# Where a block's shared chunk of edge slots stands among its parts

## The chip, the cores and the metric

The kernel runs on one core of a Trainium2 chip. The time is that of the device in microseconds (us) for one execution, the median of several runs. A profile of one execution gives the start and length of every instruction.

## The reference

Four graph layers run one after another on `x`, 16 graphs of 1024 nodes with 128 features, all with one adjacency matrix `adj` of 1024 x 1024, in which about one entry in 128 is set. Layers 0, 2 and 3 are masked attention with 8 heads of 16 features, followed by a feed-forward part; layer 1 is graph attention with one head.

```
# layers 0, 2, 3
Q, K, V = h @ Wq, h @ Wk, h @ Wv                     # 8 heads of 16
scores  = where(adj == 0, -inf, Q K^T / 4)
x = layer_norm(h + softmax(scores) V @ Wo + bo)
x = layer_norm(x + relu(x @ W1 + b1) @ W2 + b2)
# layer 1
h = x @ W
e = leaky_relu(h @ a_src [i] + h @ a_dst [j], 0.2)
y = softmax(where(adj == 0, -inf, e)) @ h + x
x = layer_norm(y)
```

## The kernel before

The kernel uses that `adj` is sparse. At the start it sorts the nodes by their number of edges and builds, for each node, the list of its neighbours. After that it never forms a 1024 x 1024 score matrix: for each node it gathers the rows of its neighbours from a table in HBM and works on these.

**Blocks.** The nodes are cut into T = 8 tiles of 128, and the 16 graphs into GR = 2 groups of 8. A block (the kernel says unit) is one layer l, one group g and one tile t; there are 4 x 2 x 8 = 64, in this order (L841). A tile has four quarters of 32 nodes. Edge slots of a quarter are gathered in chunks: one chunk covers S = 4 slots of the 32 nodes of one quarter j, so 128 rows on 128 partitions. `CAPS` (L61) holds how many slots each quarter of each tile needs. What is left over after the division by four, at most four slots in all quarters of a tile together, makes one more chunk, the shared one, called `MIX` in the code. It holds slots of two or three quarters.

**Parts.** L92 to L96 set the order in which the chunks of a tile are worked on. L94 lists the chunks (j, r) by their row r, and within a row in the order of quarters 0, 2, 1, 3; L95 makes pairs of neighbours in this list; L96 puts the shared chunk in as a part of its own, at place 3 when one counts from 0. In attention each entry of `PIECES` is a part. In layer 1 L847 packs neighbouring entries into one part as long as it has at most J = 4 chunks. Tile 0 has six entries, tiles 1 to 6 five, tile 7 four. For example, the order of tile 3 is (0,0)(2,0) | (1,0)(3,0) | (0,1)(2,1) | shared | (1,1)(3,1), and in layer 1 the first two of these go together, then the third with the shared chunk, then the last.

**The steps.** The loop at L1160 takes one part i per step and issues work for several parts, by hand (`manual_schedule`):
- L958 (`products`, VectorE): gathered keys times the queries. For ordinary parts the queries are `qr`; for the shared part they are `qx`, which L922 (`shared`) copies together from `qr` by DMA on SP's queue. There is one `qx` buffer.
- L1025 (`summed`, TensorE): part i-2's weighted values, 128 x 1024 for each chunk, are summed over slots by a matmul with a 128 x 32 matrix of marks, which writes to the 32 partitions of quarter j. L1035 to L1038 let a part wait and be summed with the next one, if both have the same row r and neither is shared.
- L981, L985 (`exponentials`, VectorE and ScalarE): scores and their exponentials. In layer 1 these are L990, L994 and L997.
- L1009 (`weighted`, VectorE): part i-1's gathered values times their weights. In attention it writes over the products, in the same buffer.
- L946 (`gathered`, GpSimd): the gathers of part i+3, one indirect DMA for each chunk, into one of four buffers `e`. The buffer is that of part i-1 and is free when L1009 of that part is done.

Product buffers `pr` are four too: L958 of a part needs the sum four parts earlier to be done. The sums of a block go to one accumulator `acc`. After the last part of a block, `divided` (L1053) sums the weights (`den`, also L1025), takes the reciprocal (L1062) and divides (L1065), which is issued in the next block's second step. Then the tails of the block (L703 for attention, L756 for layer 1: projections, layer norms, feed-forward, the table rows of the next layer) are drawn in small pieces between the steps by `others` (L1099), at an even pace. The queries of the next block (`queries`, L880) and the loads are drawn in the same way.

## Time and profile before

| what | value |
| --- | --- |
| median of 3 runs | 2261.7 us (2255.61 to 2262.03) |
| the profiled execution | 2254.23 us |
| its span, first to last instruction | 2251.9 us |
| gathers of edges, L946 | 576, mean 1483 ns on GpSimd, median 8.1 us from issue to landing |
| L958, two chunks / shared chunk | 192 of 2300 ns / 48 of 1219 ns |
| L1009, two chunks / one chunk | 256 of 2291 ns / 64 of 1217 ns |
| L981, two chunks / one chunk | 192 of 2286 ns / 48 of 1220 ns |
| L1025 into `acc` | 2624 of 608 ns, busy 519.1 us |
| DMA | 636.05 MB, mean 282 GB/s |

A row of the profile names line, engine, operation, output and inputs; a time in brackets behind a line of the timeline is the engine's idle time ahead of it, with what ended it. `PE` is TensorE, `DVE` VectorE, `ACT` ScalarE, `POOL` GpSimd and `SP` the engine that issues the other DMAs. `L1025` is busy 519.1 us though its 2624 instructions last 608 ns each, since those on different column groups run beside each other. All times in the timeline count from the start of the span.

### The profile page before, as it was taken

To read this page: it belongs to the slowest core of one execution; us is meant where nothing else is said; L and a number is where in the kernel's file an instruction comes from. 1 tells how busy PE (TensorE), PEld (TensorE's weight loads), DVE (VectorE), ACT (ScalarE), POOL (GpSimd) and SP (SyncE) were. 2 spreads that over 40 slices of the span, in tenths; PEclk is the share of its full clock that TensorE was granted. 3 is DMA by queue.
4 is the path that set the end of the run, shared out by engine and by line. 5 is a ranking of instruction groups with operands and counts; after the bars stand their busy time and mean duration, and the time that the engine had idled before them with its cause. 6 is when DMAs were issued, how large, how long until landed. Compare 5 with 4: busy or idle time off the path is not lost.

```text
span 2251.9 us, 36507 instructions
## 1 busy us (share of the span) xinstructions
PE 2043.1 (91%) x13140; PEld 1271.3 (56%) x13140; DVE 1872.9 (83%) x1472; ACT 1528.3 (68%) x5041; POOL 1016.3 (45%) x699
## 2 busy tenths in 40 slices
PE   6589999899999999998999989999999998998986
PEld 5456665555555555554556655656655555555554
DVE  7897899888887577768988889989798998888893
ACT  3346777777777655555677777777777777676765
POOL 3343445354435368884343434334444544453540
PEclk8799999999999999999999999999999998999999
DMA  7897877778788699997997978887888788687860
GB/s 254 290 323 275 298 272 279 268 263 289 284 296 272 221 341 356 360 358 291 327 329 268 318 260 302 303 313 276 284 282 305 265 286 279 225 279 271 288 227 21
DMA packets 164700, 636.05 MB, mean 282 GB/s; under 512 B 34568, under 2 KB 37384, under 8 KB 116014
## 3 DMA queue, kind: packets, MB, share of 16 engines
q0 software_dynamic: 88720, 485.08, 61.0%
q1 hardware_dynamic: 75792, 148.57, 19.1%
q8 instruction: 105, 1.72, 0.3%
q14 instruction: 83, 0.68, 0.1%
HBM read 581.08 MB, written 92.34 MB: 299 GB/s over the span
## 4 chain that ended last, share of the span: by engine, by line
PE 41%; ACT 18%; issue 16%; DVE 11%; DMA 9%; POOL 5%; POOLq 0%; DVEq 0%; ACTq 0%
PE acc L1025 9%; DMA e<-table,idx 8%; PE yps L746 5%; PE ps L576 4%; POOL e L946 4%; PE ps L646 4%; ACT qr L912 4%; PE ps L732 3%; PE ps L909 3%; DVE pr L958 3%; ACT z L624 3%; DVE sc L981 3%; DVE pr L1009 2%; PE yps L750 2%; ACT z L639 2%
## 5 line engine op out<-in xcount | busy, mean ns | idle before, releaser
L946 POOL DMA_INDIRECT e<-table,idx x576 | 854.1, 1483 | 1101.8 <-DVE pr L1009 902.1
L1009 DVE TENSOR_TENSOR pr<-e,ex 128x2048 f32<-128x2048 f32 (+1 forms) x320 | 661.6, 2076 | 46.7 <-ACT ex L985 24.9
L958 DVE TENSOR_TENSOR pr<-e,qr 128x2048 f32<-128x2048 f32 x192 | 441.6, 2300 | 132.7 <-PE acc L1025 55.7
L1025 PE MATMUL acc<-pr,marks 128*32 128x512 f32 x2624 | 519.1, 608 | 14.8 <-DVE pr L1009 10.8
L981 DVE TENSOR_REDUCE sc<-pr 128x128 f32<-128x2048 f32 (+1 forms) x240 | 497.5, 2073 | 8.0
L624 ACT ACTIVATE z<-yps,root 128x128 f32<-128x128 f32 x888 | 317.5, 388 | 35.7 <-PE yps L765 17.2
L1025 PEld LDWEIGHTS acc<-pr,marks 128*32 128x32 f32 x2624 | 107.7, 110 | 269.4 <-issue 226.7
L639 ACT ACTIVATE z<-yps,rstd 128x128 f32<-128x128 f32 x888 | 254.0, 369 | 7.2
L746 PE MATMUL yps<-W,f 128*128 128x128 f32 x1520 | 251.8, 283 | 7.3 <-ACT f L741 1.8
L741 ACT ACTIVATE f<-ps,b 128x512 f32<-128x512 f32 x190 | 129.8, 695 | 157.6 <-PE ps L732 157.2
L746 PEld LDWEIGHTS yps<-W,f 128*128 128x128 f32 x1520 | 205.0, 192 | 51.0 <-issue 25.6
L576 PE MATMUL ps<-Wkv,xT 128*128 128x256 f32 x768 | 215.0, 419 | 20.0 <-ACT xT L652 16.7
L912 ACT COPY qr<-ps 128x512 f32<-128x512 f32 x384 | 197.3, 600 | 40.6 <-PE ps L909 40.5
L909 PE MATMUL ps<-q,rep 32*128 32x512 f32 x768 | 175.3, 661 | 34.7 <-ACT q L904 33.5
L732 PE MATMUL ps<-x,W 128*128 128x512 f32 x384 | 190.4, 620 | 12.5 <-ACT x L654 12.5
L624 ACT ACTIVATION_READ_ACCUMULATOR z<-yps,root 128x1 f32 x888 | 201.7, 227 | 0.0
L646 PE MATMUL ps<-ident,z 128*128 128x128 f32 x896 | 177.5, 299 | 25.5 <-ACT z L639 20.7
L646 PEld LDWEIGHTS ps<-ident,z 128*128 128x128 f32 x896 | 115.2, 142 | 149.2 <-ACT z L639 72.1
L580 ACT COPY kv<-ps 128x512 f32<-128x512 f32 x176 | 103.2, 589 | 131.9 <-PE ps L576 119.4
L576 PEld LDWEIGHTS ps<-Wkv,xT 128*128 128x128 f32 x768 | 146.5, 205 | 76.4 <-ACT xT L652 21.1
L721 PE MATMUL yps<-Wo,oT 128*128 128x128 f32 x768 | 160.3, 292 | 8.6 <-ACT oT L652 8.5
L722 PE MATMUL yps<-centre,x 128*128 128x128 f32 x768 | 155.5, 285 | 3.6
(176 smaller groups left out, 2597.7 us busy)
## 6 DMA issues: line engine op xcount, KB each, us to landing
table<-kv SPq DMA_DIRECT2D x88, 512.0 KB, 6.5
kept<-xT SPq DMA_DIRECT2D x96, 256.0 KB, 5.4
x<-kept SPq DMA_DIRECT2D x48, 512.0 KB, 9.2
qx<-qr SPq DMA_DIRECT2D x48, 256.0 KB, 6.7
e<-table,idx POOLq DMA_INDIRECT x576, 8.1
table<-kv SPq DMA_DIRECT2D x32, 256.0 KB, 7.7
qx<-qr SPq DMA_DIRECT2D x18, 384.0 KB, 9.1
qx<-qr SPq DMA_DIRECT2D x42, 128.0 KB, 8.1
```

Of the source, the lines that this page charges most:

```text
L576: nc.tensor.matmul(ps[:, k, :], x[:, i + k, :], w[LAYERS[l][0], "Wkv"], start=True, stop=True,)
L624: nc.scalar.activation(z[:, i, :], y[:, i, :], AF.Square, scale=D**-0.5, bias=root, accum_out=total[:, i : i + 1],)
L639: nc.scalar.activation(z[:, i, :], y[:, i, :], AF.Copy, scale=rstd[:, i : i + 1])
L646: nc.tensor.transpose(ps[:, i, :], z[:, i, :], ident)
L732: nc.tensor.matmul(ps, p["W1"][:, f * P : (f + 1) * P], x1.rearrange("p g n -> p (g n)"), start=True, stop=True,)
L746: nc.tensor.matmul(ps[:, i, :], f1[:, f, i * P : (i + 1) * P], p["W2"][:, f, :], start=(f == 0), stop=False,)
L912: nc.scalar.copy(qs[u][:, j, h * GH * D : (h + 1) * GH * D], pss[j])
L946: nc.gpsimd.indirect_dma_start(out=es[i][:, k, :], out_offset=None, in_=tables[l, g][:, :], in_offset=bass.IndirectOffsetOnAxis(ap=idx[:, ...
L958: nc.vector.tensor_tensor(prs[i][0][:, :n, :], es[i][:, :n, :ROW], qx[u].rearrange("p (o c) -> p o c", o=1) if (MIX, 0) in piece else of_p ...
L981: nc.vector.tensor_reduce(sc[:, :n, :], prs[i][0][:, :n, :].rearrange("p k (a d) -> p k a d", d=HD), mybir.AxisListType.X, ALU.add,)
L1009: nc.vector.tensor_tensor(prs[i][k0 // 2][:, :m, :].rearrange("p k (a d) -> p k a d", d=d), es[i][:, k0 : k0 + m, base : base + ROW].rearr ...
L1025: nc.tensor.matmul(outs[32 * j : 32 * j + 32], marks[:, mark, :], rhss, start=(chunk == mine[0]), stop=(chunk == mine[-1]),)
```

## The change

The shared chunk goes to place 4 in place of 3, counted from 0.

```
     PIECES.append([sorted(_c[_k : _k + 2]) for _k in range(0, len(_c), 2)])
-    PIECES[_t].insert(3, [(MIX, 0)])
+    PIECES[_t].insert(4, [(MIX, 0)])
```

In tiles 1 to 6, with five entries, the shared chunk is now the last. In tile 0, with six, it is the fifth. Tile 7 has three other entries, so the shared chunk is the last of four in both kernels. Tile 3 becomes (0,0)(2,0) | (1,0)(3,0) | (0,1)(2,1) | (1,1)(3,1) | shared. In layer 1, where entries are packed up to four chunks, the numbers of chunks in the parts of tiles 1 to 6 change from 4, 3, 2 to 4, 4, 1, those of tile 0 from 4, 3, 4 to 4, 4, 3; tile 7 has 4, 3 in both. `PLACE`, the columns of the exponentials, and the start and stop flags of the sums follow the order of `PIECES`.

## Prediction

> **What bounds the kernel now.** I read the page first, then the waits, then VectorE's timeline of one block in each kind of layer, and last GpSimd's and TensorE's timelines beside it. Parts of a block are numbered 1 to 5 here; the shared chunk is part 4 now.

> From the page, its busy row and the row of the chain of waits:

> ```profile
> PE 2043.1 (91%) x13140; PEld 1271.3 (56%) x13140; DVE 1872.9 (83%) x1472; ACT 1528.3 (68%) x5041; POOL 1016.3 (45%) x699
> ...
> PE 41%; ACT 18%; issue 16%; DVE 11%; DMA 9%; POOL 5%; POOLq 0%; DVEq 0%; ACTq 0%
> ```

> No engine has the chain to itself. The view of waits names what VectorE loses (total us, times, longest):

> ```profile
> DVE sc L990 <- DMA e<-table,idx: 56.6, 34, 4.3
> DVE pr L958 <- PE acc L1025: 55.7, 32, 4.0
> ...
> DVE pr L958 <- DMA e<-table,idx: 51.7, 21, 5.5
> ```

> VectorE's timeline of an attention block of the last layer shows the last two of these in place:

> ```profile
> 1826.83 2.28 DVE L1009 TENSOR_TENSOR pr<-e,ex 128x2048 f32<-128x2048 f32 x1
> 1829.02 1.22 DVE L958 TENSOR_TENSOR pr<-e,qx 128x1024 f32<-128x1024 f32 x1
> 1830.28 1.22 DVE L981 TENSOR_REDUCE sc<-pr 128x64 f32<-128x1024 f32 x1
> 1831.41 2.35 DVE L1009 TENSOR_TENSOR pr<-e,ex 128x2048 f32<-128x2048 f32 x1
> 1833.68 2.54 DVE L958 TENSOR_TENSOR pr<-e,qr 128x2048 f32<-128x2048 f32 x1
> ...
> 1842.57 2.29 DVE L958 TENSOR_TENSOR pr<-e,qr 128x2048 f32<-128x2048 f32 x1 [2.89 <-DMA e<-table,idx]
> ```

> 1829.02 is the shared part (half as long), 1833.68 part 5, 1842.57 the next block's part 1, which waits for its gather. That gather was let go when L1009 freed its buffer at 1826.83 + 2.28 = 1829.1; it landed 13.5 us later, while the two short steps between cover 4.66 + 5.66 = 10.3. Without waits the steps of such a block (starts of L958) are 6.73 + 8.58 + 6.72 + 4.66 + 5.66 = 32.35 us; the 24 blocks of five parts in layers 2 and 3 average 36.65. So 4.3 us a block go to this gather and to the wait of part 5 for TensorE (it needs the product buffer of part 1, which the sum of parts 1 and 2 frees).

> In layer 0 the next lines are TensorE's: parts 1 and 2 are summed in one batch, part 3 alone.

> ```profile
> 607.30 1.92 PE L1025 MATMUL acc<-pr,marks 128*32 128x512 f32 x16
> ...
> 610.58 1.91 PE L1025 MATMUL acc<-pr,marks 128*32 128x512 f32 x8
> ```

> Sixteen matmuls take as long as eight: four column groups run beside each other against two. Layer 1 is different; VectorE, then GpSimd:

> ```profile
> 943.60 0.17 DVE L990 TENSOR_TENSOR sc<-e,of 128x8 f32<-128x8 f32 x1 [1.26 <-DMA e<-table,idx]
> 943.81 0.18 DVE L994 SCALAR_TENSOR_TENSOR sc<-sc 128x24 f32<-128x24 f32 x1
> 943.91 4.49 DVE L1009 TENSOR_TENSOR pr<-e,ex 128x2048 f32<-128x2048 f32 x2
> ...
> 960.54 0.17 DVE L990 TENSOR_TENSOR sc<-e,of 128x8 f32<-128x8 f32 x1 [1.10 <-DMA e<-table,idx]
> ```

> ```profile
> 949.56 0.99 POOL L946 DMA_INDIRECT e<-table,idx  x1 [0.30 <-DVE o L1065]
> 950.85 2.34 POOL L946 DMA_INDIRECT e<-table,idx  x1 [0.30 <-issue]
> 953.50 1.00 POOL L946 DMA_INDIRECT e<-table,idx  x1 [0.30 <-issue]
> ```

> These are a loop: the gather of a block's second part lands (943.60), L1009 of the first part ends (948.4) and frees a buffer, three gathers for the next block's second part go out from 949.56 to 954.5, and they land at 960.54: 16.94 us, the block's length there. In 936 to 953 the table of windows has the DMA share at 1.02 and PE busy 16.79 of 17.00.

> [...]

> **The change part by part.** Nothing is added or removed: same parts (40 and 23 per group of tiles), same instructions on VectorE, GpSimd and ScalarE, the same bytes. Tile 7 keeps its order (its list is too short), tile 0 moves the shared part from fourth to fifth of six.

> *Sums.* L1035 lets a part wait for the next if both carry the same row r and neither is shared. With the shared part out of the way parts 3 and 4 of tiles 2, 3 and 4 now meet that (r = 1 in both); tiles 0, 1, 5, 6 do not. Two batches of about 1.9 us become one: 1.9 us of TensorE less in 3 tiles x 2 groups x 3 layers = 18 blocks, 34 us in all. What falls away is the batch at 610.58. The chain of waits from 603.6 to 615.2 is ScalarE's alone (oT 0.59, x 0.62, qr 1.94, z 1.42, 1.14, 1.40 and so on), and TensorE's next work there, L732 at 612.42, needs ScalarE's x, which ends at 612.04. So the path gains 0.4 us at most in layer 0: I take 0, bounds -0.4 and 0 for 6 blocks.

> *Product buffers.* Part 5's wait (about 1.8 us) falls to the same slot, now the shared part's, which VectorE reaches 2.06 us later (6.72 for a full step against 4.66): gone. In the 18 blocks a new one comes: the next block's part 2 needs part 3's buffer, freed by the merged sum a step later. In layer 0 that sum ends where the one of the shared part ends now, at 588.5; part 2 would start there instead of 585.2 and the reciprocal, 6.8 us behind it, at 595.3 instead of 594.0. Queued behind it are the division and o, which would be ready at 597.2 and which TensorE first reads at 598.9: hidden by 1.7 us. I take 0, and +1.3 a block if that cover fails.

> *Gathers of attention.* The stall moves with the short part: now the next block's part 2 has the short steps ahead of it, 4.66 + 5.66 = 10.3 again, with a gather of two chunks 6.72 us ahead of it, as now. The query copies (L922) wait for the shared product as before and so start as close to that gather as now; SP has nothing behind them that is due sooner. Landing after 13.5 us gives the same block: 8.58 + 6.72 + 6.72 + 13.5 = 35.5 against 6.73 + 8.58 + 6.72 + 13.5 = 35.5. I take 0; the trace doesn't show a gather in the new place, so between -1.2 (landing after 12.3, if less is queued ahead) and +0.5, for 24 blocks: -29 to +12.

> *Layer 1.* Here parts are packed up to four chunks, and the packing changes from 4, 3, 2 to 4, 4, 1 (tile 0: 4, 3, 4 to 4, 4, 3) in 14 blocks. The loop's gather grows from three to four. Its slack now is the time from 948.4 to 949.56 less 0.30 of issue, about 0.9. One more issue costs 0.99 + 0.30 = 1.29, or 2.34 + 0.30 = 2.64 where a VectorE product holds it up. Loop: 16.94 - 0.9 + 1.29 to 2.64 = 17.3 to 18.7, +0.4 to +1.8 a block. I take +0.9: 14 x 0.9 = +13 us. The lower end is below nothing: sums on TensorE get 1.7 us shorter in tiles 0, 2, 3, 4 (four column groups at once), 1.7 longer in tile 1, net 2 x 3 x 1.7 = 10 us, which counts where TensorE is the chain.

> Sum for the profiled execution: 2254.2 + 13 = 2267. The median shown, 2261.7, lies 7.5 above it, so 2274.

> **Rivals.** *No change*: in layer 1 the transfers are the limit (share 1.02), the bytes are equal, and the loop only uses up slack: 2262. For it, the DMA share; against it, that the three gathers already meet VectorE waiting (943.60, 960.54). *Faster*: in layers 2 and 3 the gather of part 2 lands early. Place: the next block's second part; price: 24 x 1.2 = 29 us, so 2233; it decides once the landing takes under 13.5 us from release. For it, a landing median of 8.1; against it, the same queue ahead. *Slower by more*: the new buffer wait delays the reciprocal and with it the tails, 18 x 1.3 = 23 us on top of 13: 2298. Against it, the 1.7 us of cover. That the change does nothing is excluded, since the packing of layer 1 differs.

> **How the numbers follow.** Layer 1's loop alone 0.45 (own range 2267 to 2290), slower by more 0.13, no change 0.18, faster 0.24. A change under 0.3% (7 us) can't be told from none here. So slower 0.58, same 0.18, faster 0.24. The range reaches from 2232, into the faster case, to 2302, past the slower one.

> **What would show it.** Right: blocks of layer 1 near 18 us with L990 waiting longer for DMA; no wait of the shared part for acc; the DMA wait of attention in front of the second part, equally long; L1025 in layer 0 with 16 matmuls at the place of the shared sum. Wrong: layer 1 unchanged at 17, or attention blocks of layers 2 and 3 shorter than 35.5, or ScalarE waiting at ex for the delayed second part.

## The result and the profile after

The changed kernel takes 2271.42 us (median of 13 runs, 2261.51 to 2275.14), the kernel before 2257.4 us beside it on the same chip (13 runs, 2246.01 to 2265.78). The ratio is 1.0058, with a 95% interval of 1.0043 to 1.0074: some 13 us slower. (The ratio on record compares all the runs, and need not be the quotient of the two medians.) The forecast was 2274.0 from 2261.7, a ratio of 1.0054. The size came out; the place it was put in did not, as the sections below show. The profiled execution after took 2261.51 us (span 2259.3), the fastest of its 13, against 2254.23 (span 2251.9) before, so two profiles laid side by side show only 7.4 us of the difference.

From the page of the changed kernel, its busy row and the row of the chain of waits:

```profile
PE 2004.8 (89%) x13140; PEld 1260.5 (56%) x13140; DVE 1881.4 (83%) x1472; ACT 1530.9 (68%) x5041; POOL 964.3 (43%) x699
...
PE 37%; issue 19%; DVE 16%; ACT 15%; DMA 8%; POOL 4%; another core or an unknown queue 0%; POOLq 0%; DVEq 0%; ACTq 0%
```

TensorE has 38 us less to do than before, and yet the time is longer. The view of waits, VectorE's rows (total us, times, longest):

```profile
DVE pr L958 <- DMA e<-table,idx: 73.2, 36, 4.3
DVE sc L990 <- DMA e<-table,idx: 50.0, 21, 5.2
DVE both L1062 <- PE ps L1025: 44.2, 13, 11.7
DVE pr L958 <- PE acc L1025: 32.8, 10, 5.3
```

The gathers of attention (the first row) are waited for more often, 36 times against 21, and the product buffers (the last row) less often but longer, 10 times against 32. The two together are 106.0 us against 107.4. Layer 1's gathers (L990) are waited for less than before. VectorE's timeline of an attention block of the last layer, the one that answers to the block shown before:

```profile
1838.88 1.21 DVE L958 TENSOR_TENSOR pr<-e,qx 128x1024 f32<-128x1024 f32 x1
...
1843.52 2.28 DVE L958 TENSOR_TENSOR pr<-e,qr 128x2048 f32<-128x2048 f32 x1
...
1852.06 2.29 DVE L958 TENSOR_TENSOR pr<-e,qr 128x2048 f32<-128x2048 f32 x1 [2.81 <-DMA e<-table,idx]
```

1838.88 is the shared part, now the last of its block; part 1 of the next block (1843.52) follows at once, and its part 2 (1852.06) waits for its gather. The stall has moved by one part and kept its size: 2.81 us here, 2.89 before.

In layer 0, TensorE's timeline of the changed kernel:

```profile
573.42 1.92 PE L1025 MATMUL acc<-pr,marks 128*32 128x512 f32 x16
575.27 1.07 PE L646 MATMUL ps<-ident,z 128*128 128x128 f32 x4
576.17 0.60 PE L646 MATMUL ps<-ident,x 128*128 128x128 f32 x4
578.27 3.46 PE L732 MATMUL ps<-x,W 128*128 128x512 f32 x4 [1.50 <-ACT x L654]
...
590.38 1.92 PE L1025 MATMUL acc<-pr,marks 128*32 128x512 f32 x16
...
602.78 0.60 PE L646 MATMUL ps<-ident,o 128*128 128x128 f32 x4
```

and the same stretch of the kernel before, from the sum of part 3 on:

```profile
574.11 1.91 PE L1025 MATMUL acc<-pr,marks 128*32 128x512 f32 x8
575.95 1.98 PE L732 MATMUL ps<-x,W 128*128 128x512 f32 x4
```

573.42 is the sum of parts 1 and 2, 590.38 the merged sum of parts 3 and 4. Before, a batch of 1.91 us for part 3 alone stood between the transposes of L646 and L732. It is gone, TensorE is idle for 1.50 us in its place, and then the same four matmuls of L732 take 3.46 us where they took 1.98. The table of windows of the changed kernel shows the clock beside it (window, its length, busy us of PE, PEld, DVE, ACT and POOL with the number of instructions, granted clock of TensorE, DMA share, GB/s):

```profile
575.22:578.63 3.41, 1.91 (x13) 1.24 (x10) 3.38 (x3) 3.35 (x16) 1.45 (x1) 1.00 0.99 401
578.63:582.05 3.42, 3.42 (x7) 1.41 (x6) 3.42 (x3) 2.44 (x7) 1.52 (x3) 0.50 0.91 321
582.05:585.46 3.41, 3.41 (x28) 3.12 (x27) 3.38 (x2) 1.29 (x3) 3.10 (x2) 1.00 1.02 394
```

In the first window TensorE is busy for 1.91 of 3.41 us (0.56). In the next its granted clock is 0.50, though it has work throughout; after that it is 1.00 again.

VectorE beside it, at the start of the next block:

```profile
592.34 2.29 DVE L958 TENSOR_TENSOR pr<-e,qr 128x2048 f32<-128x2048 f32 x1 [5.13 <-PE acc L1025]
...
599.07 0.55 DVE L1062 RECIPROCAL both<-ps 128x64 f32<-128x64 f32 x1
599.65 1.29 DVE L1065 TENSOR_TENSOR o<-acc,both 128x512 f32<-128x512 f32 x2
```

That is the new wait of part 2 for the merged sum. The first of the two halves of o (L1065, x2 in 1.29 us) is ready near 600.3 and TensorE first reads it at 602.78.

### The profile page after: what moved, and what is told of

Read it like the earlier page. It is cut to its first block, busy times and chain, and to the rows that moved or that the text cites. A ratio compares the mean times of both kernels' runs of the same rounds, so it can differ in the third digit from the quotient of the medians.

```text
span 2259.3 us, 36527 instructions
## 1 busy us (share of the span) xinstructions
PE 2004.8 (89%) x13140; PEld 1260.5 (56%) x13140; DVE 1881.4 (83%) x1472; ACT 1530.9 (68%) x5041; POOL 964.3 (43%) x699
## 4 chain that ended last, share of the span: by engine, by line
PE 37%; issue 19%; DVE 16%; ACT 15%; DMA 8%; POOL 4%; another core or an unknown queue 0%; POOLq 0%; DVEq 0%; ACTq 0%
PE acc L1025 8%; DMA e<-table,idx 7%; DVE pr L1009 6%; PE yps L746 5%; PE ps L732 5%; DVE pr L958 5%; PE ps L576 4%; ACT z L624 3%; PE ps L646 3%; ACT qr L912 3%; POOL e L946 3%; DVE sc L981 2%; PE ps L909 2%; PE yps L750 2%; ACT z L639 2%
## 5 line engine op out<-in xcount | busy, mean ns | idle before, releaser
L946 POOL DMA_INDIRECT e<-table,idx x576 | 849.3, 1474 | 1155.2 <-DVE pr L1009 961.3
L1009 DVE TENSOR_TENSOR pr<-e,ex 128x2048 f32<-128x2048 f32 (+1 forms) x320 | 672.2, 2109 | 49.9 <-ACT ex L985 29.8
L958 DVE TENSOR_TENSOR pr<-e,qr 128x2048 f32<-128x2048 f32 x192 | 439.3, 2288 | 131.3 <-DMA e<-table,idx 73.2
L981 DVE TENSOR_REDUCE sc<-pr 128x128 f32<-128x2048 f32 (+1 forms) x240 | 497.5, 2073 | 8.1
L1025 PE MATMUL acc<-pr,marks 128*32 128x512 f32 x2624 | 472.7, 606 | 26.6 <-DVE pr L1009 15.7
L732 PE MATMUL ps<-x,W 128*128 128x512 f32 x384 | 210.2, 675 | 41.7 <-ACT x L654 40.8
L1025 PEld LDWEIGHTS acc<-pr,marks 128*32 128x32 f32 x2624 | 99.0, 110 | 259.0 <-issue 203.7
L646 PE MATMUL ps<-ident,z 128*128 128x128 f32 x896 | 179.2, 302 | 31.3 <-ACT z L639 24.3
L646 PEld LDWEIGHTS ps<-ident,z 128*128 128x128 f32 x896 | 118.0, 146 | 159.3 <-ACT z L639 73.3
L909 PE MATMUL ps<-q,rep 32*128 32x512 f32 x768 | 168.4, 656 | 32.8 <-ACT q L904 29.1
```

Of the source, the lines that this page charges most:

```text
L646: nc.tensor.transpose(ps[:, i, :], z[:, i, :], ident)
L732: nc.tensor.matmul(ps, p["W1"][:, f * P : (f + 1) * P], x1.rearrange("p g n -> p (g n)"), start=True, stop=True,)
L946: nc.gpsimd.indirect_dma_start(out=es[i][:, k, :], out_offset=None, in_=tables[l, g][:, :], in_offset=bass.IndirectOffsetOnAxis(ap=idx[:, ...
L958: nc.vector.tensor_tensor(prs[i][0][:, :n, :], es[i][:, :n, :ROW], qx[u].rearrange("p (o c) -> p o c", o=1) if (MIX, 0) in piece else of_p ...
L981: nc.vector.tensor_reduce(sc[:, :n, :], prs[i][0][:, :n, :].rearrange("p k (a d) -> p k a d", d=HD), mybir.AxisListType.X, ALU.add,)
L1009: nc.vector.tensor_tensor(prs[i][k0 // 2][:, :m, :].rearrange("p k (a d) -> p k a d", d=d), es[i][:, k0 : k0 + m, base : base + ROW].rearr ...
```

## The experiments

All twelve kernels carry a table `AT[l][t]` in place of the constant in L96, and `PIECES` by layer, so that lines lie up to four further down than in the profiles above (up to ten behind the filling described below). All tiles of a layer have the same place. The cuts of code show what matters of each edit and leave the rest out. Ratios are to the kernel before on the same chip, in brackets the 95% interval; as above, a ratio need not be the quotient of the two medians (for layer0_fill that would be 1.0061). "Clock" is the mean granted clock of TensorE over the runs of a kernel; in the traces of before and after it is 1.0 or 0.5 at any moment, so a mean of 0.9614 over some 2255 us is 174 us at half clock, and 0.9536 over some 2269 us is 210 us.

| kernel | median us | before us | ratio | clock |
| --- | --- | --- | --- | --- |
| the change | 2271.42 | 2257.4 | 1.0058 (1.0043 to 1.0074) | 0.9536 |
| layer1_alone | 2255.91 | 2256.47 | 0.9997 (0.9982 to 1.0013) | 0.9613 |
| attention_alone | 2272.76 | 2256.47 | 1.0057 (1.0036 to 1.0077) | 0.9532 |
| no_new_batch | 2267.77 | 2256.47 | 1.0051 (1.0031 to 1.0070) | 0.9594 |
| after_in_place | 2270.61 | 2256.47 | 1.0055 (1.0034 to 1.0076) | 0.9536 |
| after_no_seen | 2266.91 | 2250.55 | 1.0083 (1.0057 to 1.0109) | 0.9533 |
| no_batch_no_seen | 2263.82 | 2250.55 | 1.0075 (1.0056 to 1.0093) | 0.9592 |
| after_fill | 2275.98 | 2250.55 | 1.0113 (1.0096 to 1.0130) | 0.9647 |
| before_no_seen | 2248.47 | 2250.55 | 0.9993 (0.9983 to 1.0003) | 0.9630 |
| layer0_alone | 2265.41 | 2257.28 | 1.0043 (1.0025 to 1.0061) | 0.9583 |
| layer0_no_batch | 2260.56 | 2257.28 | 1.0012 (0.9998 to 1.0027) | 0.9616 |
| layer0_fill | 2271.03 | 2257.28 | 1.0041 (1.0022 to 1.0059) | 0.9579 |
| layers23_alone | 2264.21 | 2257.28 | 1.0034 (1.0018 to 1.0050) | 0.9568 |

The kernel before has a clock of 0.9614 on the chips of the first and the last group of runs, and 0.9636 on that of the middle one.

The expectations speak of theories by letter. A is the prediction: layer 1's loop of gathers costs. B: VectorE's new wait for the merged sum costs. C: the merged sum leaves TensorE idle (1.50 us above), and its clock is halved for the next window (0.50 above). D came later and has its own paragraph.

**Which layers.** The prediction put the loss into layer 1. Two kernels split the change by layer.

```
-    PIECES[_t].insert(3, [(MIX, 0)])
+    PIECES[_l, _t].insert(AT[_l][_t], [(MIX, 0)])   # AT = 4 in layer 1, else 3
```

> Only layer 1 has the shared chunk at place 4; layers 0, 2 and 3 keep place 3. Theory A (the prediction: layer 1's loop of three and then four gathers): slower than before by 0.9 us in 14 blocks, +13 us, a ratio near 1.006. Theory B (the new wait of part 2 for the merged sum, in layer 0) and theory C (the merged sum leaves TensorE idle for 1.5 us in layer 0, and its granted clock is halved for the next 3.4 us): no such batch exists here, so within 3 us of before, and the loops of layer 1 use up slack only.

```
+AT = [[4] * T, [3] * T, [4] * T, [4] * T]
```

> Layers 0, 2 and 3 have the shared chunk at place 4, layer 1 keeps place 3. Theory A: as before (within 3 us). Theories B and C: the whole loss, +8 to +16 us, with the blocks of layer 0 behind tiles 2 to 4 near 37.8 us in place of 36.5.

Layer 1 alone runs as before, and the other three layers alone have the whole loss. Theory A is refuted.

**What in the attention layers.** The merged batch has two consequences, VectorE's wait and TensorE's idle time. The first kernel takes away both, the second only the wait.

```
-        if is_attention(u) and i + 1 < len(parts) and pieces[-1][-1][0] != MIX:
+        if is_attention(u) and i + 1 < len(parts) and pieces[-1][-1][0] != MIX and r == 0:
```

> As the changed kernel, but a part waits for the next only in row 0, so parts 3 and 4 of tiles 2, 3 and 4 are summed apart as before the change. Theory A: keeps its +13 us over before. Theories B and C: both the wait of part 2 for the merged sum and the idle time of TensorE are gone, so layer 0 falls back by 6 to 11 us, to within 5 us of before, with blocks of 36.5 us.

```
 def products(i):
-        prs[i] = [prods.tile([P, 2, ROW], F32, tag="pr", name="pr")]
         nc.vector.tensor_tensor(
-            prs[i][0][:, :n, :], es[i][:, :n, :ROW],
+            es[i][:, :n, :ROW], es[i][:, :n, :ROW],
...
 def weighted(i, k0):
-        if not is_attention(u):
-            prs.setdefault(i, []).append(prods.tile([P, 2, ROW], F32, tag="pr", name="pr"))
+        prs.setdefault(i, []).append(prods.tile([P, 2, ROW], F32, tag="pr", name="pr"))
```

> As the changed kernel, but the products of L958 are written over the gathered keys, and a product buffer is taken only by L1009, 4.5 us later. The batches of sums stay as in the changed kernel. Theory B: the wait of part 2 for the merged sum shrinks from 5.1 us to about 0.6 us, so the loss goes, and since other waits for product buffers go too, the time is at or below that of before (0 to -15 us). Theory C: TensorE is idle as in the changed kernel and its clock halves as often; the blocks of layer 0 behind tiles 2 to 4 stay near 37.8 us, and the time stays 5 us or more above before. Theory A: +13 us stays.

Without the wait (after_in_place) the loss stays, as theory C has it: no product waits for `acc` any more, the ratio is 1.0055, and the clock is that of the change (0.9536). Only one of the three blocks is long in its trace, though, where theory C expected all three (see the periods below). Without the batch (no_new_batch) the clock comes most of the way back (0.9594), but the ratio is still 1.0051, which no theory expected. So there is a second part of the loss that the batch doesn't explain.

**GpSimd's addition.** A trace of the changed kernel shows one thing that neither the prediction nor the theories so far had. L1009 of part 3 starts just behind GpSimd's addition to `seen` (VectorE, then GpSimd):

```profile
574.34 2.57 DVE L1009 TENSOR_TENSOR pr<-e,ex 128x2048 f32<-128x2048 f32 x1
```

```profile
574.29 0.46 POOL L1077 TENSOR_TENSOR seen<-seen,both 128x128 f32<-128x128 f32 x1
```

Before, this L1009 took 2.32 us and the addition, which came second, 1.62. Both orders are frequent in the two traces. Of the 48 additions of attention, 41 before and 5 after start within an L1009; they take 1.50 to 1.82 us and end 0.31 or 0.32 us behind it. In 35 blocks after, the addition starts 0.02 to 0.07 us ahead of L1009; there it takes 0.46 to 0.48 us and L1009 2.57 to 2.60, against a median of 2.28 of its form. (In five more, 0.02 us ahead, the addition takes 2.61 us and L1009 2.28.) All L1009 together take 675.0 us against 664.4. Three kernels leave the addition out.

```
-        n = G * heads
-        nc.gpsimd.tensor_tensor(seen[:, :, :n], seen[:, :, :n], both, ALU.add)
```

> As the changed kernel, but GpSimd's addition of the sums of weights to seen (0.46 us, once a block) is left out, so the guard on too large values is not computed. Theory D (that addition now starts just ahead of VectorE's L1009 of part 3, which then takes 2.57 us in place of 2.32, in 37 of the 46 attention blocks with a later part): L1009 of part 3 falls back to 2.3 us or less, VectorE's busy time falls by 10 us, and of the 13 us over before 6 to 11 go. Theory C (the clock of TensorE after the idle time left by the merged sum): no change against the changed kernel, still 8 us or more above before.

> Both: parts 3 and 4 are summed apart as before the change, and the addition to seen is left out (the guard is not computed). Theories C and D together: within 3 us of before. If it stays 8 us or more above before, neither is the cause and the order of the parts itself costs.

> The kernel before, without the addition to seen (the guard is not computed). Theory D: there that addition waits for VectorE (1.62 us long) and holds nothing up, so within 3 us of before. If it is faster by 5 us or more, the addition costs in both kernels and theory D explains less of the difference.

L1009 falls to 663.8 us in the changed kernel, as expected, but the loss stays: 1.0083, at least 1.0057, on this chip, where the unaltered change was not run. VectorE's 10.6 us were not what set the time. Theory D, which expected 6 to 11 us of the 13 to go, is refuted, and no_batch_no_seen (1.0075) again shows the second part.

**Layer 0 against layers 2 and 3.** Three kernels more.

```
+AT = [[4] * T, [3] * T, [3] * T, [3] * T]
```

> Only layer 0 has the shared chunk at place 4. If the loss is layer 0's, the ratio is that of the whole change, 1.004 to 1.006 (+9 to +13 us), with L732 of the tails at 3.46 us and blocks of 37.8 us behind tiles 2 to 4 of the second group. If the loss comes from layers 2 and 3, within 3 us of before.

The same with `r == 0` in L1035, as in no_new_batch:

> As the run with layer 0 alone, but parts 3 and 4 are summed apart as before the change. Theory C (idle TensorE, then half the clock): L732 at 1.98 us, blocks of the second group at 36.5 us, 4 to 6 us less than layer 0 alone. If the order of the parts alone costs in layer 0, no less.

```
+AT = [[3] * T, [3] * T, [4] * T, [4] * T]
```

> Only layers 2 and 3 have the shared chunk at place 4. If the loss is layer 0's: within 3 us of before. If the order of the parts costs in the gathers' loop too: +4 to +8 us, with the blocks of layer 3 longer by 0.3 to 0.5 us on average.

Layer 0 costs 1.0043 and without its merged batch 1.0012, with the clock back at that of before (0.9616). So in layer 0 the batch is the larger part: some 5 us between the medians of these two kernels and 7 us between their ratios, of a loss of 8 to 10. Layers 2 and 3 cost 1.0034 on their own.

**Filling the gap.** If TensorE's idle time is what costs, work put into it must bring the clock back. At the place where part 3 was summed, matmuls with a weight of zeros are added to `acc`.

```
             if v == u and first[1] == r and first[0] != MIX and i - 1 not in prs:
+                for h in range(HF if r else 0):
+                    for j in [*range(J)] * 2:      # layer0_fill: range(J)
+                        nc.tensor.matmul(
+                            accums[u][32 * j : 32 * j + 32, h, :], none, marks[:, :16, :],
+                            start=False, stop=False,
+                        )
                 return
```

> As the changed kernel, but at the place where part 3 was summed on its own sixteen matmuls with a weight of zeros are added to acc, 1.9 us of TensorE that change no value. Theory C: TensorE is no longer idle there, its clock stays full, the blocks of layer 0 behind tiles 2 to 4 go back from 37.8 to 36.6 us, and the time falls by 5 to 8 us though work is added. Theory D: no change (within 3 us), or slower where TensorE is the chain.

> As the run with layer 0 alone, with the batch of parts 3 and 4 kept, but at the place where part 3 was summed on its own eight matmuls with a weight of zeros are added to acc (1.8 us of TensorE, no value changed; the earlier filling was 3.64 us, twice the gap). Theory C: work is added and time falls, by 3 to 6 us against layer 0 alone; L732 at 1.98 us, blocks near 36.6 us, no halved clock in the second group. Theory B (VectorE's wait for the merged sum): no gain, since that wait stays; blocks stay at 37.8 us.

The first filling took 3.64 us, twice the gap, so it adds time of its own and can't decide. The second fits. TensorE's timeline of layer0_fill (L1029 stands for L1025, L1044 for the filling, L736 for L732):

```profile
540.07 1.92 PE L1029 MATMUL acc<-pr,marks 128*32 128x512 f32 x16
...
543.35 1.92 PE L1044 MATMUL acc<-marks,none 128*32 128x512 f32 x16
545.21 1.98 PE L736 MATMUL ps<-x,W 128*128 128x512 f32 x4
```

and VectorE's in the same block (L962 stands for L958):

```profile
557.91 2.29 DVE L962 TENSOR_TENSOR pr<-e,qr 128x2048 f32<-128x2048 f32 x1 [5.19 <-PE acc L1029]
```

L732 takes 1.98 us again. The next sum of parts 1 and 2 starts at 576.74, 36.67 us after 540.07, as in the kernel before (36.60) and although VectorE's wait for the merged sum is as long as ever (5.19 us). In the block behind it, though, another window is short of work. The table of windows of layer0_fill there:

```profile
594.25:597.66 3.41, 2.23 (x15) 1.34 (x11) 3.06 (x2) 2.93 (x13) 0.25 (x1) 1.00 0.99 382
597.66:601.08 3.42, 3.42 (x14) 0.94 (x16) 3.42 (x2) 1.55 (x6) 0.00 (x0) 0.50 0.97 340
```

TensorE is busy for 0.65 of it, the clock is halved for the next, and the period is 38.52 us. The time as a whole didn't come back (1.0041, clock 0.9579), which was not expected; its 22 runs reach from 2254.55 us at a clock of 0.965 to 2277.62 us at 0.951. What the filling shows is local.

**The periods.** From the traces, the time in layer 0's second group from the sum of parts 1 and 2 of one block to that of the next, in brackets the us at half clock in it:

| kernel | tile 1 to 2 | 2 to 3 | 3 to 4 | 4 to 5 | 5 to 6 |
| --- | --- | --- | --- | --- | --- |
| before | 36.59 (0) | 36.60 (0) | 36.48 (0) | 36.59 (0) | 36.70 (0) |
| layer0_no_batch | 36.51 (0) | 36.63 (0) | 36.63 (0) | 36.62 (0) | 36.73 (0) |
| the change | 36.53 (0) | 37.66 (3.4) | 37.76 (3.4) | 37.97 (3.4) | 36.92 (0) |
| layer0_alone | 36.51 (0) | 37.55 (3.4) | 37.55 (3.4) | 37.55 (3.4) | 36.91 (0) |
| after_in_place | 36.53 (0) | 36.75 (0) | 38.61 (3.4) | 36.97 (0) | 36.77 (0) |
| layer0_fill | 36.54 (0) | 36.67 (0) | 38.52 (3.4) | 36.80 (0) | 37.31 (0) |
| after_fill | 36.54 (0) | 38.28 (0) | 38.28 (0) | 38.28 (0) | 36.91 (0) |

Leaving the last row aside, a period without a halved window is 36.5 to 37.3 us, whether VectorE waits for the merged sum or not; one with a halved window is 37.5 to 38.6. In after_in_place TensorE's gap of 1.5 us ahead of L732 stands in all three blocks with a merged sum, L732 behind it takes 1.98 or 1.99 us each time, and two of the three periods are 36.75 and 36.97 us: without a halved window the gap costs 0.2 to 0.4 us there, against 1.0 to 1.4 us in the change. The last row has no halved window, and its periods are longer by the 1.7 us that its filling has too much; that fits TensorE's own sequence setting the pace here.

No run was faster than the kernel before beyond its interval; before_no_seen, at 0.9993, is not told apart from it and leaves work out.

## Why the prediction was right in size and wrong in place

*Layer 1, forecast +13 us: the term that failed.* Measured alone it is 0.9997 (-4 to +3 us). The loop is there in the block that was read. In the second group, VectorE's timeline of the changed kernel has the last piece of a block's second part at

```profile
949.60 0.17 DVE L990 TENSOR_TENSOR sc<-e,of 128x16 f32<-128x16 f32 x1 [2.85 <-DMA e<-table,idx]
...
967.41 0.17 DVE L990 TENSOR_TENSOR sc<-e,of 128x16 f32<-128x16 f32 x1 [3.81 <-DMA e<-table,idx]
```

17.81 us apart, within the forecast 17.3 to 18.7 and 0.87 above the 16.94 of the same block before, where +0.9 was worked out. But 16.94 was the shortest of its neighbours: counted alike, tiles 2 to 4 take 17.6, 16.9 and 18.7 us before and 18.2, 17.8 and 18.8 after. Over seven profiles of either order these three tiles average 17.8 and 18.0 us, and 17.0 and 17.8 if a block is counted from its first part; so the loop costs 0.1 to 0.8 us where it holds, depending on the point one counts from. What was wrong above all is the factor of 14. The other tiles are not in that loop: counted from their first parts, tiles 0 to 6 of both groups average 19.82 and 20.00 us, and tile 7's two blocks are 1.1 and 1.8 us shorter. The sum of the layer is 312.8 and 312.3 us. The total wait of L990 fell (56.6 to 50.0), where the prediction had it grow.

*Sums, forecast 0 (-0.4 to 0): the step that failed.* The batch falls away where expected, and L732 starts 0.28 us sooner behind the sum of parts 1 and 2 (4.85 against 5.13 us), inside the bounds. The sentence on ScalarE's chain holds as well. But the step took work removed from TensorE to be worth nothing at worst, and had no term for the clock. The work left a gap of 1.5 us, seen in the total of the waits of L732 for ScalarE's x, before and after:

```profile
PE ps L732 <- ACT x L654: 12.5, 10, 1.7
```

```profile
PE ps L732 <- ACT x L654: 40.8, 27, 1.7
```

17 waits more, of 1.66 us on average. In the three such blocks of layer 0's second group the window behind the gap is at half clock, and each of these periods is 1.0 to 1.4 us longer. Layer 0 run alone has a ratio of 1.0043 with the batch and 1.0012 without it.

*Product buffers, forecast 0, +1.3 a block if the cover fails.* The new wait came as worked out, in part 2, and the reciprocal moved up directly behind L1009. The cover held: o is ready 2.4 us before TensorE reads it (600.3 and 602.78 above), and the period of 36.67 us under a wait of 5.19 us shows that it costs nothing there. The rival that was slower by this wait named 1.3 us in each of 18 blocks; blocks longer by about that much did appear in layer 0, from another cause.

*Gathers of attention, forecast 0.* Inside the bounds where it was worked out: the 24 blocks of tiles 1 to 6 in layers 2 and 3, counted from first part to first part, average 36.54 us in six profiles with the old order and 36.48 in six with the new; counted from the second parts, where the wait now stands, 36.52 and 36.70. But the two layers as a whole cost 1.0034, between 4 and 11 us. In the same profiles their four groups change by +3.1, -0.8, +1.4 and +4.8 us, so it lies mostly in the first and the last. One place stands out, a block of tile 0, which has six parts and stood outside the 24 that were priced. In the last group, from its first part to the next block's, it takes 46.3 to 48.3 us in the six old profiles and 49.3 to 51.1 in all eight with the new order there, those without the batch included. Part 1 of the next block, before and after:

```profile
1955.02 2.28 DVE L958 TENSOR_TENSOR pr<-e,qr 128x2048 f32<-128x2048 f32 x1
```

```profile
1961.52 2.29 DVE L958 TENSOR_TENSOR pr<-e,qr 128x2048 f32<-128x2048 f32 x1 [4.03 <-DMA e<-table,idx]
```

The wait for a gather stands here now, right behind the two short steps; the profile of before has none here, and a wait of 1.28 us for `acc` in tile 0's fifth part. No run tests this place alone. The clock is lower too when layers 2 and 3 are changed alone (0.9568), but no_new_batch has lost the batch and keeps 1.0051. What the rest of these layers' loss is, and how much of it is the clock, stays open.

*The whole in terms of the clock.* Over the change's 13 runs TensorE is at half clock for 210 us. Beside them the clock of the kernel before was not recorded; in the three groups of runs of the experiments it is 174, 164 and 174 us. Against 174 that is 36 us more. Over 75 runs of the kernel before on one chip, a microsecond more at half clock goes with 0.36 us more time (correlation 0.73), over 26 runs on another with 0.23 (0.60), over 27 on the third with 0.10 (0.30). By these slopes 36 us would be worth 4 to 13 of the 13 us. This is an estimate from a correlation; the cause is shown block by block only for layer 0's second group.

The range and the sign held by luck: two errors offset each other, +13 us in a layer that costs nothing and 0 in layers that cost 13. The forecast's own signs said so: layer 1's blocks were not near 18 us throughout, and the wait of L990 fell.

## What to carry to other kernels

Taking work off a busy engine is not free of risk when what remains is a gap (here 1.5 us, and blocks 1.0 to 1.4 us longer): look at which step of the clock record, 3.41 us here, loses TensorE work, and how far its busy share falls. In the two traces 59 of 79 full-clock steps with a share under 0.60 were followed by half clock, and 8 of 1129 with a higher one (the last section has the counts). A loop seen in two or three blocks is not the layer; before a price per block is multiplied, the same wait has to be found in every block that it is charged to. And an idle time shown before an instruction (here 5.1 us of VectorE for a buffer) is a cost only if the next reader of its result waits.

## What the runs showed of the hardware

Here half clock followed a window in which TensorE was merely less busy, not idle: 1.91 us of work in 3.41, then 0.50 (575.22 and 578.63 above). In the two profiles, taken in steps of 3.413 us from the first change of clock, windows at full clock were followed by one at half clock so often:

| busy share of TensorE in the window | followed by half clock | by full clock |
| --- | --- | --- |
| under 0.45 | 31 | 2 |
| 0.45 to 0.60 | 28 | 18 |
| 0.60 to 0.70 | 3 | 45 |
| 0.70 to 0.90 | 5 | 214 |
| over 0.90 | 0 | 862 |

Between 0.45 and 0.60 both outcomes are common (28 and 18), so the share alone doesn't decide. That it matters where on the grid a gap of 1.5 us falls is an estimate, from two figures: periods of 36.6 us are 10.7 steps of 3.413, so the place changes from block to block, and of the gaps in after_in_place none halved the clock for L732 (1.98 or 1.99 us) where all three of the change did. It would also fit the spread between executions of one kernel, whose time goes with their clock as said above; it was not tested apart.
